# An attention kernel's last addition of an image ahead of the next image's sums, with its tiles moved by 32 bytes

## The chip, the cores and the metric

The kernel runs on one core of a Trainium2 chip. The metric is the device time of one execution in microseconds. A core has a matrix engine (TensorE, PE in the profile; its weight loads are listed as PEld), a vector engine (VectorE, DVE), a scalar engine (ScalarE, ACT), GpSimd (POOL) and SyncE (SP). Each engine works through its own list of instructions, and they wait for each other through semaphores. SBUF is the working memory, of 128 partitions; PSUM holds TensorE's results.

## The reference

Four images `x` of 64 × 64 positions and 256 channels go through one self-attention layer, in float32:

```python
q = einsum('bwhc,cd->bwhd', x, Wq) + bq        # 256 -> 128
k = einsum('bwhc,cd->bwhd', x, Wk) + bk        # 256 -> 128
v = einsum('bwhc,cd->bwhd', x, Wv) + bv        # 256 -> 256
pq, pk, pv = (t.reshape(B, -1, N) for t in (q, k, v))    # N = 4096
energy = einsum('bcn,bcm->bnm', pq, pk)
out = einsum('bcm,bnm->bcn', pv, softmax(energy, axis=-1))
return gamma * out.reshape(B, W, H, C) + x
```

The output has the shape of `x`, (4, 64, 64, 256).

## The kernel before

Matrix products of the attention run in `float32r`, TensorE's one-pass float32 format, with each operand split into parts so that the sum of three products keeps the precision. The projections and the transposes run in plain float32. For one image the kernel projects 16 tiles of `x` to `q`, `k` and `v`, then takes 128 steps `u`: 16 groups `g` of 256 columns, with 8 steps `t` in a group. In a step TensorE multiplies the energies of a step ahead (12 matmuls) and attends (24 matmuls into the banks `a0`, `a1` and `bb`).

When a group ends, its result must be finished: the two accumulators are copied out on ACT (L385), the sums of the softmax are turned into factors, `bb` is added (L400), the sum is scaled (L403), transposed by TensorE (L411), added to `x` and stored. This is a generator, so that its parts fall between the instructions of the steps that follow. A call of `proceed` lets every open generator do one part, up to its next `yield`.

```python
def attend(b, u):
    ...                                     # 24 matmuls into acc[0], acc[1], bb
    if t == NU - 1 and (b, g) != (B - 1, NG - 1):
        o = now["o"] = work.tile([P, NJ, C + 2], F32, tag="o", ...)
        for j in range(NJ):                 # L385, ACT
            nc.scalar.activation(o[:, j, :], acc[j], AF.Identity, scale=1.0 + E)

def finish(b, g, o, bb, xr):
    yield
    yield
    nc.vector.tensor_copy(zall[:, b * NG + g, :], o[:, :, C])                 # L398, DVE
    r, _ = factors(b, g, gam1)                                                # L390, L391, DVE
    nc.vector.tensor_tensor(o[:, :, :C], o[:, :, :C], bb, ALU.add)            # L400, DVE
    yield
    for j in range(NJ):                                                       # L403, ACT
        nc.scalar.activation(o[:, j, :C], o[:, j, :C], AF.Identity, scale=r[:, j : j + 1])
    yield
    yield
    tp = ps_t.tile([P, 2, NB], F32, tag="t", ...)
    ...                                     # L411: 4 transposes on TensorE
    yield
    nc.vector.tensor_tensor(xr, xr, tp, ALU.add)                              # L415, DVE
    nc.gpsimd.dma_start(ov[b, g], xr)
```

The projection of an image: `transposed` turns a tile of `x` (L124, TensorE) and copies it to `xts` (L130, ACT); `project_qk` multiplies (L137, TensorE), adds the biases (`qks`, L146, DVE), and makes three parts `f` of `k` (L263 on ACT, L265 twice on DVE). The loop over the images, with the passage from one to the next:

```python
for b in range(B):
    pr = images[b]
    if b == 0:
        ...                                 # the first image's first tiles
    for i in range(1, NI):
        if i == 3:
            now["banks"] = outputs
        if i + 1 < NI:
            pr.transposed(i + 1)
        while i == 1 and active:            # the rest of the last group's finish
            proceed()
        begin(b, i)
        project_qk(b, i)
        ...
        project_v(b, i - 1)
        proceed()
    project_v(b, NI - 1)
    for u in range(STEPS):
        ...                                 # a step; images[b + 1].transposed(0) in its last but one
        attend(b, u)
        if ...:
            ...
        elif t == NU - 1:
            start(finish(b, g, now["o"], now["bb"], loads.pop((b, "x", g))))
        proceed()
    if b + 1 < B:
        images[b + 1].transposed(1)
        project_qk(b + 1, 0)
```

Tiles get their SBUF addresses in the order in which the pools are opened. Small pools named `pad` hold nothing and move what comes after them:

```python
xpool, xtpool, qkv = pool("xpool", 3), pool("xtpool", 3), pool("qkv", 1)

pool("pad", 1).tile([P, 16], F32, name="pad")
ppool = pool("ppool", 2)                    # probabilities: x, y, h, l, d
pool("pad2", 1).tile([P, 112], F32, name="pad2")
work = pool("work", 2)                      # qks, v4, qr, q, o, r
pool("pad3", 1).tile([P, 48], F32, name="pad3")
kpool = pool("kpool", 3)                    # f, k
```

The constants (`ident`, the weights and biases, `zall`) lie in front of `xpool`.

Of the kernel before, what the change touches and what calls it, by code (L numbers as in the profile page):

```python
# [9 lines left out]
F32 = mybir.dt.float32  # L10
# [10 lines left out]
def kernel(  # L21
# [38 lines left out]
    P = 128  # L60
# [19 lines left out]
    def load_x(pool, b, g):  # L80
        t = pool.tile([P, 2, XB], F32, tag="x", name=f"x_{b}_{g}")
        nc.sync.dma_start(t, xv[b, g])
        return t
# [117 lines left out]
    with ExitStack() as fast:  # L201
        fast.enter_context(tc.manual_schedule())
        pool = lambda name, bufs, **kw: fast.enter_context(
            tc.tile_pool(name=name, bufs=bufs, **kw)
        )
        xpool, xtpool, qkv = pool("xpool", 3), pool("xtpool", 3), pool("qkv", 1)

        pool("pad", 1).tile([P, 16], F32, name="pad")
        ppool = pool("ppool", 2)
        pool("pad2", 1).tile([P, 112], F32, name="pad2")  # L210
# [25 lines left out]
        def proceed():  # L236
            for pieces in list(active):
                if next(pieces, StopIteration) is StopIteration:
                    active.remove(pieces)

        def image(b):
            def xt_out(i):
                return xtpool.tile([P, KC, 2, P], F32, tag="xt", name=f"xts_{b}_{i}")

            def qk_out(i):
                now["qk"] = work.tile([P, 2, 2 * C2], F32, tag="qk", name=f"qks_{b}_{i}")
                return ((now["qk"], 0),)

            def v_out(i):
                now["v4"] = work.tile([P, KC, C], F32, tag="v4", name=f"v4_{b}_{i}")  # L250
                return now["v4"], bv4_sb, 1.0 / E

            images.append(Projection(b, xpool, lambda: next(now["banks"]), xt_out, qk_out, v_out))

            for g in range(NG):
                qd[b, g] = dram.tile([P, NJ, P], F32, tag=f"qd{g}", name=f"qd_{b}_{g}")
            for t in range(NU):
                kf[b, t] = dram.tile([P, 2, 2, 3 * P], F32R, tag=f"kf{t}", name=f"kf_{b}_{t}")

        def halved(f, x):  # L260

            h = f[:, :, 0, :]
            nc.scalar.activation(h, x, AF.Identity, scale=UPPER / 64)  # L263
            for j, s, op in ((1, -64.0, ALU.add), (2, 64.0 * (1.0 + E), ALU.subtract)):
                nc.vector.scalar_tensor_tensor(  # L265
                    f[:, :, j, :], h.bitcast(F32), s, x, ALU.mult, op
                )

        def project_qk(b, i):
            images[b].qk(i)  # L270
            x = now["qk"]
            for s in range(2):
                nc.gpsimd.dma_start(qd[b, i // 2 + NG // 2 * s][:, i % 2, :], x[:, s, :C2])  # L273
            f = kpool.tile([P, 2, 3, P], F32R, tag="f", name=f"f_{b}_{i}", bufs=2)
            halved(f, x[:, :, C2:])
            nc.gpsimd.dma_start(kf[b, i // 2][:, i % 2], f.rearrange("p s j d -> p s (j d)"))

        def project_v(b, i):
            images[b].v(i)
            units[b, "v4", i] = now["v4"]  # L280
            if i < NI - 2:
                halve_v(b, i)
# [12 lines left out]
        def load_q(b, g):  # L295
            t = work.tile([P, NJ, P], F32, tag="qr", name=f"qr_{b}_{g}", bufs=1)
            nc.sync.dma_start(t, qd[b, g])
            loads[b, "qr", g] = t
# [12 lines left out]
        def energy(b, u, k):  # L311

            g, t = divmod(u, NU)
            if k == 0:
                x = ppool.tile([P, 4, NB], F32, tag="x", name=f"x_{b}_{u}", bufs=3)
                y = ppool.tile([P, 4, NB], F32, tag="y", name=f"y_{b}_{u}")
                units[b, u] = x, y
            x, y = units[b, u]
            q, kt = loads[b, "q", g], loads[b, "k", u]
            sa = ps_s.tile([P, 2, NJ, P], F32, tag="a", name=f"sa_{b}_{u}_{k}")  # L320
            sb = ps_s.tile([P, 2, NJ, P], F32, tag="b", name=f"sb_{b}_{u}_{k}")
            for i in range(2):
                for to, f, first, last in ((sa, 0, True, False), (sa, 1, False, True), (sb, 2, True, True)):
                    nc.tensor.matmul(  # L324
                        to[:, i], kt[:, 2 * k + i, f, :], q[:, f], start=first, stop=last
                    )
            for to, sp, scale in ((x, sa, (1.0 + E) / E), (y, sb, -1.0 / E)):
                nc.scalar.activation(  # L328
                    to[:, 2 * k : 2 * k + 2, :],
                    sp.rearrange("p i j d -> p i (j d)"),  # L330
                    AF.Exp,
                    scale=scale,
                )
# [12 lines left out]
        def halves(b, u):  # L346
            x, h = units[b, u]
            l = ppool.tile([P, 4, NB], F32R, tag="l", name=f"l_{b}_{u}")
            nc.vector.tensor_tensor(l, x, h.bitcast(F32), ALU.subtract)  # L349

            d = ppool.tile([P, 4, NB], F32R, tag="d", name=f"d_{b}_{u}")
            nc.vector.scalar_tensor_tensor(  # L352
                d, h.bitcast(F32), 1.0 + E, x, ALU.mult, ALU.subtract
            )
            units[b, u] = h, l, d
# [106 lines left out]
        def begin(b, i):  # L462

            if i == 5:
                load_q(b, 0)
            if i == 9:
                halve_q(b, 0)
            if i in (4, 6, 8):
                load_k(b, i // 2 - 2)
            if i >= 10:  # L470
                energy(b, (i - 10) // 2, i % 2)
            if i in (12, 14):
                join(b, i // 2 - 6)
            if i in (13, 15):
                upper(b, i // 2 - 6)
                load_k(b, i // 2 - 3)

        image(0)
# [3 lines that stand above are left out]
                now["banks"] = energies  # L482
                pr.transposed(0)
                pr.transposed(1)
                project_qk(b, 0)
# [5 lines that stand above are left out]
                while i == 1 and active:  # L491
# [3 lines that stand above are left out]
                if i == NI - 1:  # L495
                    halves(b, 0)
# [4 lines that stand above are left out]
                g, t = divmod(u, NU)  # L501
                ahead = u + LOOK
                if ahead // NU + 1 < NG and ahead % NU == 3:
                    load_q(b, ahead // NU + 1)
                if u == STEPS - NU and b + 1 < B:
                    image(b + 1)
                if u >= STEPS - 3 and b + 1 < B:
                    now["banks"] = energies
                    if u == STEPS - 3:
                        images[b + 1].load(0)  # L510
                    elif u == STEPS - 2:
                        images[b + 1].transposed(0)
                if t == NU - 3:
                    loads[b, "x", g] = load_x(xpool, b, g)
                for k in range(2):
                    if ahead < STEPS:
                        energy(b, ahead, k)
                    if k == 0 and u + 2 < STEPS:
                        join(b, u + 2)
                        upper(b, u + 2)  # L520
                load_k(b, ahead + 2)
                proceed()
                if u + 1 < STEPS:
                    halves(b, u + 1)
                if ahead // NU + 1 < NG and ahead % NU == 5:
                    halve_q(b, ahead // NU + 1)

                if u in (1, 3):
                    halve_v(b, NI - 2 + u // 2)
                attend(b, u)  # L530
                if (b, u) == (B - 1, STEPS - 1):
                    finish_last(b, g, loads.pop((b, "x", g)))
                elif t == NU - 1:
                    start(finish(b, g, now["o"], now["bb"], loads.pop((b, "x", g))))
                proceed()
            if b + 1 < B:
                images[b + 1].transposed(1)
                project_qk(b + 1, 0)

    NB = 512  # L540
    NG = N // NB
# [3 lines left out]
    with tc.If(nc.values_load(again[0:1, 0:1]) > 0), ExitStack() as general:  # L545
        pool = lambda name, bufs, **kw: general.enter_context(
            tc.tile_pool(name=name, bufs=bufs, **kw)
        )
# [125 lines left out]
```

## Time and profile before

| | |
|---|---|
| time, median of 3 | 2474.3 us (2473.92 to 2475.12) |
| span of the profiled execution | 2471.3 us |
| attention matmuls: energies (L324) and attend (L374), float32r | 6,144 and 12,288 |
| mean duration of one attend matmul, `a` from `vh`; `bb` | 283 ns; 279 ns |
| projection matmul records (L137, L158), float32 | 512 and 512 |
| HBM read, written | 445.25 MB, 50.33 MB |
| mean busy share of the DMA engines over the slices | 0.6 to 0.7 in most |

Matmuls are pipelined, so the duration of one (279 ns) is not what it adds to the time: the distance from one start to the next is about 113 to 125 ns. A float32 projection matmul has two records. The three passages between images lie at about 616, 1229 and 1846 us of the span.

### The profile page before, as it was taken

To read this page: it belongs to the slowest core of one execution; us is meant where nothing else is said; L and a number is where in the kernel's file an instruction comes from. 1 tells how busy PE (TensorE), PEld (TensorE's weight loads), DVE (VectorE), ACT (ScalarE), POOL (GpSimd) and SP (SyncE) were. 2 spreads that over 40 slices of the span, in tenths; PEclk is the share of its full clock that TensorE was granted. 3 is DMA by queue.
4 is the path that set the end of the run, shared out by engine and by line. 5 is a ranking of instruction groups with operands and counts; after the bars stand their busy time and mean duration, and the time that the engine had idled before them with its cause. 6 is when DMAs were issued, how large, how long until landed. Compare 5 with 4: busy or idle time off the path is not lost.

```text
span 2471.3 us, 50024 instructions
## 1 busy us (share of the span) xinstructions
PE 2447.6 (99%) x19982; PEld 2412.5 (98%) x19982; DVE 2095.9 (85%) x2314; ACT 1805.7 (73%) x3201; POOL 425.7 (17%) x781
## 2 busy tenths in 40 slices
PE   9999999999999999999999999999999999999998
PEld 8999999999899999999989999999998999999998
DVE  5888888888698888888769888888876988888887
ACT  5777777776677777777657777777766777777775
POOL 4211111111411111111131111111114111111110
PEclk9999999999999999999999999999999999999999
DMA  7666666664766666666477666666647766666663
GB/s 234 220 204 204 208 206 205 198 211 144 237 215 198 206 210 204 207 202 207 142 226 216 204 201 209 204 211 201 207 141 224 224 205 198 208 206 205 209 201 111
DMA packets 137408, 498.92 MB, mean 202 GB/s; under 512 B 15536, under 2 KB 57264, under 8 KB 137168
## 3 DMA queue, kind: packets, MB, share of 16 engines
q0 software_dynamic: 92320, 453.17, 58.8%
q1 hardware_dynamic: 44304, 42.22, 5.6%
q8 instruction: 160, 2.62, 0.4%
q14 instruction: 80, 0.66, 0.1%
q10 hardware_dynamic: 544, 0.26, 0.0%
HBM read 445.25 MB, written 50.33 MB: 201 GB/s over the span
## 4 chain that ended last, share of the span: by engine, by line


## 5 line engine op out<-in xcount | busy, mean ns | idle before, releaser
L328 ACT ACTIVATE x<-sa 128x512 f32<-128x512 f32 x1024 | 612.9, 599 | 494.9 <-PE sa L324 491.7
L338 DVE TENSOR_TENSOR x<-x,y 128x1024 f32<-128x1024 f32 x512 | 626.4, 1223 | 188.0 <-ACT y L328 188.0
L324 PE MATMUL sa<-q,k 128*128 128x256 f32 x4096 | 736.6, 279 | 1.1 <-ACT x L328 1.1
L352 DVE SCALAR_TENSOR_TENSOR d<-h,x 128x1024 fp32r<-128x1024 f32 x512 | 624.4, 1219 | 0.0
L349 DVE TENSOR_TENSOR l<-x,h 128x1024 fp32r<-128x1024 f32 x512 | 624.3, 1219 | 0.0
L324 PEld LDWEIGHTS sa<-q,k 128*128 128x128 f32 x4096 | 619.5, 188 | 2.4 <-ACT x L328 1.9
L328 ACT ACTIVATE y<-sb 128x512 f32<-128x512 f32 x1024 | 614.6, 600 | 0.0
L374 PE MATMUL a<-vh,h 128*128 128x258 f32 x4096 | 574.4, 283 | 0.0
L374 PE MATMUL a<-vl,l 128*128 128x258 f32 x4096 | 572.8, 282 | 0.0
L324 PE MATMUL sb<-q,k 128*128 128x256 f32 x2048 | 567.6, 277 | 0.0
L343 ACT ACTIVATE h<-x 128x1024 fp32r<-128x1024 f32 x512 | 544.6, 1064 | 23.1 <-DVE x L338 19.2
L374 PE MATMUL bb<-vd,d 128*128 128x256 f32 x4096 | 558.6, 279 | 0.0
L308 POOL DMA_DIRECT2D k<-kf x512 | 280.0, 547 | 1575.4 <-PE sb L324 1550.4
L374 PEld LDWEIGHTS a<-vl,l 128*128 128x128 f32 x4096 | 525.3, 189 | 0.0
L374 PEld LDWEIGHTS a<-vh,h 128*128 128x128 f32 x4096 | 522.9, 189 | 0.0
L374 PEld LDWEIGHTS bb<-vd,d 128*128 128x128 f32 x4096 | 515.1, 188 | 0.0
L324 PEld LDWEIGHTS sb<-q,k 128*128 128x128 f32 x2048 | 384.5, 188 | 0.9 <-ACT y L328 0.8
L137 PE MATMUL qk<-wqk_sb,xts 128*128 128x256 f32 x512 | 124.4, 387 | 0.0
L158 PE MATMUL v<-xts,wv_sb 128*128 128x256 f32 x512 | 121.2, 381 | 0.0
L158 PEld LDWEIGHTS v<-xts,wv_sb 128*128 128x128 f32 x512 | 98.2, 192 | 13.7
L137 PEld LDWEIGHTS qk<-wqk_sb,xts 128*128 128x128 f32 x512 | 94.5, 194 | 10.7
L273 POOL DMA_DIRECT2D qd<-qks x128 | 69.1, 544 | 187.3 <-DVE qks L146 178.1
(56 smaller groups left out, 869.7 us busy)
## 6 DMA issues: line engine op xcount, KB each, us to landing
k<-kf POOLq DMA_DIRECT2D x512, 768.0 KB, 4.7
x<-in_x_dram SPq DMA_DIRECT2D x128, 256.0 KB, 3.4
kf<-f POOLq DMA_DIRECT2D x64, 384.0 KB, 3.7
out_dram<-x POOLq DMA_DIRECT2D x63, 256.0 KB, 2.5
qd<-qks POOLq DMA_DIRECT2D x128, 64.0 KB, 2.8
qr<-qd SPq DMA_DIRECT2D x64, 128.0 KB, 2.6
wv_sb<-in_L_conv_Wv_dram POOLq DMA_DIRECT2D x1, 256.0 KB, 5.8
out_dram<-x SPq DMA_DIRECT2D x1, 256.0 KB, 3.7
```

What stands on the lines that cost most here:

```text
L137: nc.tensor.matmul(qk[:, s, :], self.xt[i][:, k, s, :], wqk_sb[:, k, :], start=(k == 0), stop=(k == KC - 1),)
L158: nc.tensor.matmul(vp[:, eh, :], wv_sb[:, k, eh * P : (eh + 1) * P], self.xt[i][:, k].rearrange("p s a -> p (s a)"), start=(k == 0), stop= ...
L273: nc.gpsimd.dma_start(qd[b, i // 2 + NG // 2 * s][:, i % 2, :], x[:, s, :C2])
L308: nc.gpsimd.dma_start(t.rearrange("p (i s) f d -> p i s (f d)", s=2), kf[b, u % NU])
L324: nc.tensor.matmul(to[:, i], kt[:, 2 * k + i, f, :], q[:, f], start=first, stop=last)
L328: nc.scalar.activation(to[:, 2 * k : 2 * k + 2, :], sp.rearrange("p i j d -> p i (j d)"), AF.Exp, scale=scale,)
L338: nc.vector.tensor_tensor(x, x, y, ALU.mult)
L343: nc.scalar.activation(h, units[b, u], AF.Identity, scale=UPPER)
L349: nc.vector.tensor_tensor(l, x, h.bitcast(F32), ALU.subtract)
L352: nc.vector.scalar_tensor_tensor(d, h.bitcast(F32), 1.0 + E, x, ALU.mult, ALU.subtract)
L374: nc.tensor.matmul(out_, left[:, i, j * P : (j + 1) * P], right[:, m, : out_.shape[1]], start=(t == i == 0 and (left is h or left is d and ...
```

## The change

Two calls of `proceed` are added at the passage to the next image: one before the next image's tile 1 is transposed, one after its tile 0 is projected. With the first, the part of `finish` that makes the factors and adds the shared bank `bb` stands ahead of the next image's bias sums in DVE's list. With the second, the scaling stands ahead of the following copy in ACT's list. The purpose is that DVE does this work while it has nothing else to do, so that the last output transposes can run sooner. The `while` loop in the next image then finds two parts fewer to do.

Besides, a pool `pad0` of 8 floats for each partition is opened ahead of `xpool`. It moves every tile from `x` on by 32 bytes, while the constants stay.

```diff
         pool = lambda name, bufs, **kw: fast.enter_context(
             tc.tile_pool(name=name, bufs=bufs, **kw)
         )
+
+
+        pool("pad0", 1).tile([P, 8], F32, name="pad0")
         xpool, xtpool, qkv = pool("xpool", 3), pool("xtpool", 3), pool("qkv", 1)
-
         pool("pad", 1).tile([P, 16], F32, name="pad")
         ppool = pool("ppool", 2)
         pool("pad2", 1).tile([P, 112], F32, name="pad2")
@@ -534,8 +536,10 @@
                     start(finish(b, g, now["o"], now["bb"], loads.pop((b, "x", g))))
                 proceed()
             if b + 1 < B:
+                proceed()
                 images[b + 1].transposed(1)
                 project_qk(b + 1, 0)
+                proceed()
```

## The prediction

> **What bounds the kernel now.** I read the page first, its busy shares and its clock row:
>
> ```profile
> PE 2447.6 (99%) x19982; PEld 2412.5 (98%) x19982; DVE 2095.9 (85%) x2314; ACT 1805.7 (73%) x3201; POOL 425.7 (17%) x781
> ...
> PEclk9999999999999999999999999999999999999999
> ```
>
> TensorE has work for 2447.6 of 2471.3 us, and the other engines have slack. So a gain comes either from the 23.7 us in which TensorE idles or from faster matmuls. The page's chain of waits is empty here, so next I asked for TensorE's own waits. Two of the answer's lines are shown here; the others are a first load, a start, four short waits for ACT and one wait at the very end:
>
> ```profile
> PE ot L411 <- ACT o L403: 10.0, 3, 3.3
> ...
> PE sa L324 <- ACT x L328: 1.1, 4, 0.3
> ```
>
> Three waits of 3.3 us, one at each passage from one image to the next, are the one large idle time that the program order can change. The timeline of the first passage shows what TensorE, DVE and ACT do there (columns: start, duration, engine, line, operation, and in brackets the idle time before it with what ended it):
>
> ```profile
> 616.12 0.60 PE L124 MATMUL xt<-ident,x 128*128 128x128 f32 x4
> 616.55 1.89 PE L137 MATMUL qk<-wqk_sb,xts 128*128 128x256 f32 x8
> 618.28 0.60 PE L124 MATMUL xt<-ident,x 128*128 128x128 f32 x4
> 622.21 0.95 PE L411 MATMUL ot<-ident,o 128*128 128x128 f32 x4 [3.33 <-ACT o L403]
> ```
>
> ```profile
> 618.48 0.69 DVE L146 TENSOR_TENSOR qks<-qk,bqk_sb 128x512 f32<-128x512 f32 x1 [6.00 <-PE qk L137]
> 619.66 0.76 DVE L265 SCALAR_TENSOR_TENSOR f<-f,qks 128x256 fp32r<-128x256 f32 x2 [0.48 <-ACT f L263]
> ...
> 620.88 0.68 DVE L400 TENSOR_TENSOR o<-o,bb 128x512 f32<-128x512 f32 x1
> ```
>
> ```profile
> 614.91 0.87 ACT L385 ACTIVATE o<-a 128x258 f32<-128x258 f32 x2 [3.69 <-PE a L374]
> 616.75 0.59 ACT L130 COPY xts<-xt 128x512 f32<-128x512 f32 x1 [0.98 <-PE xt L124]
> 619.21 0.42 ACT L263 ACTIVATE f<-qks 128x256 fp32r<-128x256 f32 x1 [1.87 <-DVE qks L146]
> 619.53 0.57 ACT L130 COPY xts<-xt 128x512 f32<-128x512 f32 x1
> 621.65 0.91 ACT L403 ACTIVATE o<-o,r 128x256 f32<-128x256 f32 x2 [1.55 <-DVE o L400]
> ```
>
> The old image's `o` is ready at 615.78 (L385) and its `bb` at about 616.3, when the last attend matmuls end. DVE has been idle since 612.5, but its next instruction in order is `qks` of the new image, which waits for TensorE until 618.48. The small operations on `zall` and `r` and the addition `o+bb` (L400) stand behind it and start only at 620.34. L403 scales `o` on ACT after that, and TensorE's output transposes wait for L403.
>
> At the second passage the same gap has a sequel. TensorE's timeline there reads:
>
> ```profile
> 1235.56 1.31 PE L411 MATMUL ot<-ident,o 128*128 128x128 f32 x4 [3.33 <-ACT o L403]
> 1236.65 3.62 PE L137 MATMUL qk<-wqk_sb,xts 128*128 128x256 f32 x8
> 1240.07 2.78 PE L158 MATMUL v<-xts,wv_sb 128*128 128x256 f32 x8
> ```
>
> The eight `qk` records take 3.62 us there against 1.89 at the first passage: the trace's clock record grants half speed for 6.8 us after the second gap, for 3.4 us after the third, and none is lost after the first.
>
> **What the Trainium skill says.** "TensorE: Matmul & The Clock Gate", table at its head: DVE and ACT run a strict first-in-first-out queue. The trace agrees: L398 to L400 had their inputs by about 616.3 and stood 4 us behind `qks`. The same page, "Part 1: The HAM clock gate", has TensorE's clock gate watch windows of 3.4 us and halve the clock after an idle one. The gaps here are 3.33 us, and two of three were followed by half speed in pieces of 3.4 us: the trace agrees in kind. "SBUF — State Buffer", "Operand start alignment", gives only the legality of a start address and says that it timed nothing, so no page tells what 32 bytes are worth for speed.
>
> **The order, worked out.** The compared instruction orders show TensorE's, the DMA queues' and GpSimd's sequences unchanged. At each of three passages the DVE operations L398, L390, L391 and L400 move ahead of `qks` and the two `f`, and on ACT the two L403 move ahead of the copy of `xts` that starts at 619.53. Nothing is added or removed.
>
> - DVE: the `zall` copy starts at about 615.8, when L385 ends. Copy, reciprocal and product took 0.54 us (620.34 to 620.88), so L400 starts when both these and `bb` are done, about 616.4, and ends about 617.1. `qks` still starts at 618.48: no collision.
> - ACT: L403 now stands behind `f` (L263) and ahead of the `xts` copy. It still comes after `f`, which comes after `qks`: so it doesn't start at 617.3 but takes the place of the copy, 619.53. It started at 621.65, so it is 2.12 us earlier.
> - TensorE: the output transposes follow L403's start by 0.56 us (622.21 − 621.65), so they start at 620.09. The transposes before them end at 618.88 (622.21 − 3.33), so a gap of 1.21 us remains out of 3.33.
> - The moved `xts` copy runs from 620.44 to 621.0. The next `qk` doesn't use it (it uses the tile copied at 616.75), and the one that does comes some 4 us later. Its banks are free. So TensorE keeps the 2.12 us.
>
> Three passages by 2.12 give 6.4 us. The clock: at the second passage the output transposes cost 1.31 − 0.95 = 0.36, `qk` 3.62 − 1.89 = 1.73 and `v` 2.78 − 1.89 = 0.89, together 2.98 us. At the third the timeline has 1.07 and 3.50 for the first two, 0.12 + 1.61 = 1.73. A gap of 1.2 us is barely a third of such a window, so I expect no half clock: 4.7 us more. Together 11.1 us, and 2474.3 − 11.1 = 2463.2.
>
> **The 32 bytes, worked out as far as they go.** From the programs' addresses: `x` of the image, `xts`, `vh`, `vl`, `vd`, `q` start at 32 modulo 64 and move to 0 modulo 64 (one of the two buffers of `o` goes the other way); the probabilities' tiles and `k` go from 96 to 128 modulo 256. Constants (`wqk_sb`, `wv_sb`, `ident`) stay. Start to start, the 18,432 fp32r matmuls take 117.0 ns on average by the trace, with a floor of 113: an excess of 4 ns, or 74 us in all. That excess is not noise. At one place of the eight-step cycle the same matmul repeats within 1 or 2 ns in nearly all of its 64 occurrences, while neighbouring places lie anywhere from 113 to 125. So something fixed, such as addresses, sets it, and a shift could redraw it.
>
> What speaks for little effect: the relations among all moved tiles are kept. Rows of `vh` are 1040 bytes apart, so as moving operands they already start at 0, 16, 32 and 48 modulo 64, and their means are 120.0, 119.4, 120.4 and 119.8 ns: alignment modulo 64 buys nothing there. For fp32, `v` has weights at 0 modulo 64 and `qk` at 32, and both take 216 ns. Not covered is an fp32r weight load, which before the change always starts at 32 modulo 64. I put the shift at −2 us, with about ±8 (a tenth of the excess either way): a guess with its size from the trace. The prediction is 2461 us.
>
> **Rivals.**
> - The shift decides. If aligned weights brought all fp32r matmuls near the floor, up to 74 us would go and the time be near 2400. For it: the fixed pattern of 113 to 125 ns. Against it: the two comparisons above. An unlucky redraw by +1 ns per matmul costs 18 us, which makes 2481.
> - The wait only changes its name. L403 waits for `f`, hence for `qks`, hence for `qk`: that is why I don't take the whole 3.33 us. If the moved copy held up `qk` after all, TensorE would wait 0.2 us at each passage, and 2462 results.
> - The gap is closed wholly: 3 × 1.21 = 3.6 us more, 2457. ACT's order speaks against it.
> - The half clock stays after a short gap, or falls elsewhere: up to 4.7 us back, 2466.
>
> **Range and chances.** The order's part lies between 6 and 12 us, the shift's mostly between −10 and +6. Together 2449 to 2469 should hold the time 8 times in 10. 2% is 49 us: faster by that needs nearly the whole matmul excess to go (0.03), slower needs almost 3 ns more on every matmul (0.01).
>
> **What would show it right or wrong.** In the changed kernel TensorE's waits for L403 should total about 3.6 us in three, with L400 starting about 0.6 us after L385's end and L403 right behind `f`. The clock row should show no half speed between images. The means of the large matmul groups and their start-to-start times should stay within 0.5 ns: a step of the mean pitch by 1 ns is 18 us and would make the shift the main cause. A new wait at `qk` or at the later `xts` would show the order's part wrong.

## The result and the profile after

The changed kernel takes 2464.24 us (median of 4 runs, 2463.92 to 2465.16), the kernel before 2474.11 us (4 runs): a ratio of 0.9961 with a 95% interval of 0.9943 to 0.9978. That is 9.9 us less, where about 13 were predicted: 11.1 for the order and 2 for the shift. It lies inside the predicted range of 2449 to 2469.

Line numbers of the passages are two higher in the changed kernel (L403 is now L405, and so on). TensorE's waits by the changed kernel's profile (us in total, times, longest):

```profile
PE ot L413 <- ACT o L405: 3.6, 3, 1.2
```

Before it stood at 10.0 us. The first passage in the changed kernel's timeline, TensorE's, DVE's and ACT's:

```profile
619.00 1.89 PE L137 MATMUL qk<-wqk_sb,xts 128*128 128x256 f32 x8
620.73 0.60 PE L124 MATMUL xt<-ident,x 128*128 128x128 f32 x4
622.52 0.95 PE L413 MATMUL ot<-ident,o 128*128 128x128 f32 x4 [1.20 <-ACT o L405]
623.30 1.89 PE L137 MATMUL qk<-wqk_sb,xts 128*128 128x256 f32 x8
```

```profile
618.24 0.17 DVE L400 COPY zall<-o 128x2 f32<-128x2 f32 x1 [3.36 <-ACT o L387]
...
618.76 0.69 DVE L402 TENSOR_TENSOR o<-o,bb 128x512 f32<-128x512 f32 x1
620.93 0.69 DVE L146 TENSOR_TENSOR qks<-qk,bqk_sb 128x512 f32<-128x512 f32 x1 [1.48 <-PE qk L137]
```

```profile
617.33 0.88 ACT L387 ACTIVATE o<-a 128x258 f32<-128x258 f32 x2 [3.73 <-PE a L376]
619.20 0.59 ACT L130 COPY xts<-xt 128x512 f32<-128x512 f32 x1 [0.99 <-PE xt L124]
621.65 0.42 ACT L265 ACTIVATE f<-qks 128x256 fp32r<-128x256 f32 x1 [1.87 <-DVE qks L146]
621.98 0.89 ACT L405 ACTIVATE o<-o,r 128x256 f32<-128x256 f32 x2
622.77 0.56 ACT L130 COPY xts<-xt 128x512 f32<-128x512 f32 x1
```

DVE adds `bb` at 618.76, some 2 us ahead of the new sums. The sum is ready at 619.45, but ACT takes it up only at 621.98: ahead of the scaling in ACT's list stands `f`, for which ACT waits 1.87 us, until the new sums are there. So 1.2 us of the wait stay. The second passage, where the kernel before ran at half speed:

```profile
1233.82 0.95 PE L413 MATMUL ot<-ident,o 128*128 128x128 f32 x4 [1.19 <-ACT o L405]
1234.61 1.89 PE L137 MATMUL qk<-wqk_sb,xts 128*128 128x256 f32 x8
```

The eight `qk` records take 1.89 us here, full speed; they took 3.62 before. In the changed kernel's profile no passage is followed by half speed.

The two profiled spans differ by less than the timed runs: 2471.3 and 2463.2, 8.1 us. Matched matmul by matmul, the changed kernel's execution loses 2.3 us in its first 11.5 us, where its projection records start 0.43 us apart instead of 0.21 (the clock at the start of the program). It then gains 6.4 us at the passages (three times 2.13) and 4.6 us by the half speed that is gone; 0.7 us is lost in small steps elsewhere. A start of that kind came and went from profile to profile.

### The profile page after: what moved, and what is told of

Its sections match the earlier page's. It is cut to its first block, busy times and chain, and to the rows that moved or that the text cites. A ratio compares the mean times of both kernels' runs of the same rounds, so it can differ in the third digit from the quotient of the medians.

```text
span 2463.2 us, 50024 instructions
## 1 busy us (share of the span) xinstructions
PE 2445.7 (99%) x19982; PEld 2411.2 (98%) x19982; DVE 2096.1 (85%) x2314; ACT 1804.0 (73%) x3201; POOL 425.7 (17%) x781
## 4 chain that ended last, share of the span: by engine, by line
## 5 line engine op out<-in xcount | busy, mean ns | idle before, releaser
L158 PE MATMUL v<-xts,wv_sb 128*128 128x256 f32 x512 | 120.3, 379 | 0.0
```

The costliest lines, as they stand in the source:

```text
L158: nc.tensor.matmul(vp[:, eh, :], wv_sb[:, k, eh * P : (eh + 1) * P], self.xt[i][:, k].rearrange("p s a -> p (s a)"), start=(k == 0), stop= ...
```

## Experiments

Theory A: the order does it all, the shift nothing. Theory B: the shift has a share of its own, through the addresses of TensorE's operands. Times are compared with runs of the kernel before in the same batch. Those had a median of 2475.3 us in the batch of the first four experiments, 2474.9 in that of the next four, and 2474.6 in the last.

### Each part alone

The order without the shift, and then the shift without the order, both as edits of the changed kernel:

```diff
-        pool("pad0", 1).tile([P, 8], F32, name="pad0")
```

> The two added calls without the 32 bytes: all tiles lie where they lay before. Theory A (the order does it all: a wait of 3.33 us falls to 1.2 us at each of three passages, and the half clock after them goes): 2464.2 us, within 1 us of the changed kernel, with three waits of the output transposes for ACT of 1.2 us each. Theory B (the shift has a share): it differs from 2464.2 by what the shift is worth, over 2 us.

Measured: 2464.19 us, ratio 0.9955 (0.9941 to 0.9968), and three waits of 1.2 us. Theory A's number.

```diff
             if b + 1 < B:
-                proceed()
                 images[b + 1].transposed(1)
                 project_qk(b + 1, 0)
-                proceed()
```

> The 32 bytes without the two calls. Theory A: as the kernel before, 2474.1 us within 1 us, three waits of 3.3 us, and every group of attention matmuls at the same mean distance from start to start as before (117.0 ns where none waits). Theory B: it differs by over 2 us, and the distances with it.

Measured: 2476.68 us, ratio 1.0007 (0.9999 to 1.0015). Its waits are those of the kernel before:

```profile
PE ot L413 <- ACT o L405: 10.0, 3, 3.3
```

The median is 1.4 us above the kernel before, where less than 1 was expected; the interval of the ratio includes 1. Its profile has half speed for 3.4 us after all three gaps. Start to start, the attention matmuls that don't wait (under 140 ns) take 117.05 ns on average, against 117.03 before. To see whether a cost of 1.4 us is real, the changed kernel and its twin without the shift were run side by side once more:

> The changed kernel once more, on the same chip as its twin without the 32 bytes in the next run. Both theories of the order: about 2464.2 us. If the shift is worth nothing, the two lie within 1 us of each other; the first comparison of the shift alone gave +1.4 us with an interval that holds zero, and a true cost of that size would show again here.

> The two calls without the 32 bytes, beside the changed kernel. No effect of the shift: the same within 1 us. A cost of the shift of about 1.4 us: this one faster by that.

Measured: 2464.67 us (ratio 0.9958, 0.9945 to 0.9972) with the shift and 2464.03 us (0.9956, 0.9942 to 0.9969) without. The 1.4 us don't come back; what is left, 0.6 us, is less than the spread of either (1.6 and 2.6 us). The traces show below where such a cost arises.

### What remains of the wait

The second added call taken away again:

```diff
                 project_qk(b + 1, 0)
-                proceed()
```

> The changed kernel without its second added call: DVE's addition is early, but ACT's scaling stands behind the copy of the transposed tile (0.57 us) again. Theory A (the rest of the wait is ACT's order): the three waits grow from 1.2 to about 1.77 us, the time by 1.7 us to 2465.9. Rival (DVE's early addition alone is enough, ACT's place is of no account): as the changed kernel, 2464.2.

Measured: 2468.01 us, ratio 0.9972 (0.9962 to 0.9982). At the first passage, TensorE and ACT:

```profile
621.74 0.94 PE L413 MATMUL ot<-ident,o 128*128 128x128 f32 x4 [1.68 <-ACT o L405]
```

```profile
620.39 0.42 ACT L265 ACTIVATE f<-qks 128x256 fp32r<-128x256 f32 x1 [1.87 <-DVE qks L146]
620.72 0.57 ACT L130 COPY xts<-xt 128x512 f32<-128x512 f32 x1
621.18 0.91 ACT L405 ACTIVATE o<-o,r 128x256 f32<-128x256 f32 x2
```

The wait is 1.68 us, near the 1.77 expected, since the copy stands ahead of the scaling again. So the second call is worth 0.5 us of wait at each passage, 1.4 us in all. The time, though, is 3.8 us above the order alone in the same batch, where 1.7 was expected. At the second passage this profile shows half speed again (3.17 us for eight `qk`):

```profile
1233.66 0.94 PE L413 MATMUL ot<-ident,o 128*128 128x128 f32 x4 [1.68 <-ACT o L405]
1234.44 3.17 PE L137 MATMUL qk<-wqk_sb,xts 128*128 128x256 f32 x8
```

That costs 1.28 us on these `qk` and 0.45 us on the `v` that follow, 1.7 us together. It happened at one of three passages in the profiled execution. The other runs fit: all nine have a mean granted clock (the share of full speed that TensorE was granted over the span) of 0.997 or 0.998, and all five of the order alone have 0.999. A thousandth of the span is 2.5 us, so half speed can make up the rest of the difference; the record doesn't say at which passages it fell in each run.

The other way round, the second call is put ahead of the projection, so that ACT scales before it makes `f`:

```diff
                 images[b + 1].transposed(1)
-                project_qk(b + 1, 0)
                 proceed()
+                project_qk(b + 1, 0)
```

> The second added call moved ahead of the projection of the next image's tile 0: ACT scales before it makes f, which waits for the new projection's sums. Theory A: the scaling starts at 0.1 us after the addition or the copy of the transposed tile and is done before TensorE has finished the following transposes; the three waits of 1.2 us go wholly, 3.6 us less than the changed kernel, 2460.6. Rival (another wait takes its place, at the projection that follows or at the bank of the transposes): TensorE's waits at the passages stay above 0.3 us each and the gain is under 2.5 us.

Measured: 2460.23 us (2457.64 to 2461.07), ratio 0.9939 (0.9926 to 0.9953), 4.0 us under the order alone in the same batch. TensorE's list of waits has no entry for the output transposes at the passages any more. The first passage, TensorE and ACT:

```profile
618.63 0.60 PE L124 MATMUL xt<-ident,x 128*128 128x128 f32 x4
619.07 0.60 PE L413 MATMUL ot<-ident,o 128*128 128x128 f32 x4
619.50 1.89 PE L137 MATMUL qk<-wqk_sb,xts 128*128 128x256 f32 x8
```

```profile
617.10 0.58 ACT L130 COPY xts<-xt 128x512 f32<-128x512 f32 x1 [1.00 <-PE xt L124]
617.59 0.91 ACT L405 ACTIVATE o<-o,r 128x256 f32<-128x256 f32 x2
619.56 0.42 ACT L265 ACTIVATE f<-qks 128x256 fp32r<-128x256 f32 x1 [1.07 <-DVE qks L146]
```

The scaling fills time in which ACT waited, and the transposes follow without a gap. They also take 0.43 us from start to the next `qk` instead of 0.79: the second of the four transposes starts 0.11 us after the first, against 0.41 before, so it seems to wait no longer for the second scaling. The same order without the 32 bytes:

> The best order found, the second added call ahead of the projection, without the 32 bytes. If the shift is worth nothing: 2460 us as with it, within 1.5 us, and no wait of the output transposes at the three passages.

Measured: 2459.12 us (2457.55 to 2459.45), ratio 0.9937 (0.9920 to 0.9953). With the shift it was 2460.23 us in another batch; the two ratios, 0.9937 and 0.9939, can't be told apart.

### Why the shift does next to nothing

For each of the three attend groups (`vh`, `vl`, `vd`), each step of the cycle of eight and the first seven of its eight matmuls, I took the median distance to the next start over its 64 occurrences: 168 places, with the kernel before as the standard. In the changed kernel all 168 agree within 1 ns. The question is then whether addresses matter at all. Further edits of the changed kernel, one for each run:

```diff
-        pool("pad0", 1).tile([P, 8], F32, name="pad0")
+        pool("pad0", 1).tile([P, 40], F32, name="pad0")     # shift_160: all by 160 bytes
-        pool("pad", 1).tile([P, 16], F32, name="pad")
+        pool("pad", 1).tile([P, 24], F32, name="pad")       # pad_24; pad_8 has 8 instead
-    VC = C + 4
+    VC = C + 2                                              # vc_258
```

> The changed kernel with all tiles from x on moved by 160 bytes instead of 32: every relation among the moved tiles is kept, every absolute address is another. If only the relations count, all 168 compared places of the attend matmuls keep their medians within 1 ns and the time is 2464 to 2466 us. If the change's 32 bytes were harmless by luck, places move and the time goes up by over 3 us.

> The changed kernel with the empty pool between the v tiles and the probabilities enlarged from 64 to 96 bytes: now the weights of the attend matmuls move by 32 bytes against their moving operand, which the change itself never does. If the fixed pattern of 113 to 125 ns from start to start comes from where the two operands lie against each other, the medians of many of its 192 places move by over 2 ns; if it comes from something else (the order of the instructions), they stay, and the time is 2464 to 2466 us.

> The changed kernel with the empty pool between the v tiles and the probabilities cut from 64 to 32 bytes, the opposite of the run with 96. If the relation of the two operands counts: under half of the 168 places stay within 1 ns, and the time leaves 2464 us by over 3 us, more probably upward, since the pools had been chosen by their times. If 96 bytes were bad for another reason (an end of memory, one tile's place): 2464 to 2466 us and the places stay.

> The changed kernel with rows of vh and vl of 258 instead of 260 elements, 1032 bytes apart instead of 1040: [...]everything after it moves up. If addresses set the pattern, the places of vh and vl get other medians while those of vd keep theirs; if the 258 columns themselves cost the 120 ns against 113 to 116 for 256, the mean of vh and vl stays at 119.5 to 120.

| kernel (one run each, the first: median of 4) | us | places within 1 ns of before | over 2 ns off | mean distance, not waiting |
|---|---|---|---|---|
| changed kernel | 2464.2 | 168 | 0 | 117.06 ns |
| all by 160 bytes | 2464.8 | 168 | 0 | 117.05 ns |
| 96 bytes between `vd` and the probabilities | 2487.0 | 44 | 99 | 118.25 ns |
| 32 bytes between them | 2491.0 | 41 | 95 | 118.59 ns |
| rows of `vh`, `vl` of 258 | 2473.0 | 45 | 96 | 117.47 ns |

The four single runs have a mean granted clock of 0.999, and the widest set of runs of one kernel, 21 of the kernel before, spans 5.1 us.

Moving everything by the same amount leaves every place as it was. Resizing `pad` moves the weights (`h`, `l`, `d`), and all else behind it, `q` and `k` too, by 32 bytes against `x`, `xts` and the moving operands (`vh`, `vl`, `vd`) ahead of it; that costs 23 to 27 us. With 32 bytes between, the tiles behind `pad` lie exactly where they lay in the kernel before, and the tiles ahead of it where they lie in the changed kernel, so neither place is bad by itself. The fixed pattern does come from addresses, from where things lie against each other, and the change keeps those relations. That the two which count are weights and moving operand is the nearest reading; other pairs across `pad` were not tested apart.

How directly this holds can be seen in single rows. One step further, `vh` and `vl` are read 2 × 1040 = 2080 bytes on, which is 2048 + 32. With 96 bytes between, the weights lie 32 bytes further on, so step `t` stands as step `t − 1` did, but for 2048 bytes. The medians for `vh` (ns, first seven matmuls):

```
changed kernel, t = 0:   114 119 123 120 117 122 121
96 bytes,       t = 1:   114 119 123 120 118 122 121
changed kernel, t = 2:   120 122 113 119 122 120 125
96 bytes,       t = 3:   120 122 113 119 122 120 125
```

The same fits for `vl`. With 96 bytes, four of the seven steps that have a predecessor fit so (`t` = 1, 3, 4 and 5, at least six of seven places within 1 ns), and `t` = 2, 6 and 7 don't. With 32 bytes `t = 0` takes the changed kernel's `t = 1` in all seven places of `vh` and of `vl`, but no other step fits in both. Two steps taken at random agree in about two of seven places. So a relation modulo 2048 seems to be a part of the rule, and it isn't the whole. What happens in the memory was not found out.

One part surprised. The energies' operands `q` and `k` move together in all these runs, yet they slow down as well. A step and the energies after it in the changed kernel, then the same with 32 bytes between (columns as above; the distance between starts is what counts):

```profile
327.06 1.08 PE L376 MATMUL bb<-vd,d 128*128 128x256 f32 x8
327.98 0.39 PE L326 MATMUL sa<-q,k 128*128 128x256 f32 x2
...
329.34 1.11 PE L376 MATMUL a<-vh,h 128*128 128x258 f32 x8
```

```profile
328.53 1.11 PE L376 MATMUL bb<-vd,d 128*128 128x256 f32 x8
329.48 0.41 PE L326 MATMUL sa<-q,k 128*128 128x256 f32 x2
...
330.90 1.13 PE L376 MATMUL a<-vh,h 128*128 128x258 f32 x8
```

The eight `bb` take 0.92 us in the first and 0.95 in the second, the twelve energies 1.36 us (113 ns each) and 1.42 us (118 ns each). In the run with 32 bytes `q` and `k` lie at the very addresses of the kernel before, so their own place is not the reason. The changed kernel's trace has both paces too; its next step:

```profile
331.25 1.11 PE L376 MATMUL bb<-vd,d 128*128 128x256 f32 x8
332.20 0.40 PE L326 MATMUL sa<-q,k 128*128 128x256 f32 x2
...
333.61 1.12 PE L376 MATMUL a<-vh,h 128*128 128x258 f32 x8
```

Here the twelve take 1.41 us. They do so after step `t = 3` in all 64 cases, whichever buffers of `q` and `k` they read, and the last `bb` of that step run at 118 ns as well. After other steps with nothing in between, the last `bb` and the energies run at 113 in nearly all cases (after `t = 1` at 118). So the pace of the matmuls ahead carries on into the energies. Transposes in between break it: in the kernel before, the energies behind `t = 1` take 113 ns in all 60 cases in which output transposes stand in between, and 118 in three of the four without.

So the cost of moving tiles against each other doesn't stay where the relation changed. By the mean distances, of about 22 us with 96 bytes the `bb` matmuls bear 11, the energies 10 and `vl` 1; of about 28 us with 32 bytes the energies bear 17, `bb` 9 and `vl` 2. `vh` bears none: its places change, and their mean stays at 119.8 ns. The carried pace would also tell why `vd`'s places moved in the run with rows of 258 (33 of 56 by over 2 ns) though `vd` and `d` moved by the same 512 bytes there: my expectation that they keep theirs was wrong.

It is also where the shift does cost something. The output transposes read `ident`, which the shift doesn't move. The 60 groups of energies behind them take 75.0 us together in each of the four profiles without the shift, and 75.7 in each of the five with 32 bytes: 28 of the 60 groups are slower. That is about 0.65 us, near the 0.6 that the runs side by side left. That `ident`'s relation is the reason is inferred.

## Why the prediction was right, and where not

**The bound and the wait.** Right. TensorE's three waits fell from 3.33 to 1.20 us each, where 1.21 was worked out. DVE's addition starts 0.55 us after the accumulators are copied out, where 0.6 was expected, and the scaling follows `f` without idle time. From the second transposes of `xt` to the next `qk`, the first passage took 4.72 us before (618.28 to 623.00) and takes 2.57, so TensorE keeps the gap's 2.13 us; no wait at `qk` or at the later `xts` took its place. The kernel before had there:

```profile
623.00 1.89 PE L137 MATMUL qk<-wqk_sb,xts 128*128 128x256 f32 x8
```

The step that saw ACT's order as the new limit is what the two moved calls show: 1.68 us of wait with the copy ahead of the scaling, none with the scaling ahead of `f`.

**The clock.** Right in kind. Eight profiles with gaps of 1.2 us have no half speed after any of 24 gaps; the kernel before has it after two of three gaps of 3.3 us and the shift alone after three of three; gaps of 1.7 us have it after one of three. "TensorE: Matmul & The Clock Gate", "Part 1: The HAM clock gate", in the Trainium skill gives a window of 3.4 us and an idle one as the cause. The window agrees: inside every trace the clock record changes at steps of 3.41 us. But no gap here is as long as a window, so a window idle in part was enough. Laid over these steps, half speed began behind all five windows in which a gap took 1.97 to 2.86 us, behind one of the three in which it took 1.67 to 1.75 us, and behind none in which it took less. Once it stayed for a second window, which isn't explained. So the length alone doesn't decide: the first gap of the kernel before fell on a boundary, 1.75 us on one side and 1.58 on the other, and escaped by its place.

The 4.7 us were read from one execution, but the timed runs fit them. The mean granted clock of a run is 0.996 or 0.997 in 36 of 37 runs of the kernel before beside the experiments, and 0.998 or 0.999 in all 19 of the changed kernel and of the order alone. The means, 0.9963 and 0.9986, differ by some 5 to 6 us of the span (an estimate from rounded figures).

**The order's sum.** 11.1 us predicted. The order alone measured 11.1 us in the batch of the first four experiments (2475.29 − 2464.19) and 10.8 in the second (2474.86 − 2464.03); the changed kernel had 9.9 and 10.2. That the first agrees to a tenth is partly luck, since the batches differ by more and the clock's part came from one execution.

**The shift.** The term of the sum that was mis-sized: −2 us, with −10 to +6 in the range, was put down, and it is about +0.65 us by the traces, and 0.6 by the medians of the runs side by side, which is within their spread. The prediction had the argument that decides it, "the relations among all moved tiles are kept", and set a guess beside it all the same, because the excess of 74 us over the floor could be redrawn. It can, by 23 to 27 us with 32 bytes, but in these runs only where tiles moved against each other. The comparison of alignments, too, was thinner than it looked: it used `vh` alone, and `vl`, with the same four starts modulo 64, has 119.9, 119.9, 117.9 and 120.3 ns. The mean distance moved by 0.03 ns where a limit of 0.5 had been set.

**The rivals.** None came: the shift didn't decide, no new wait arose, and in the profiles of the changed kernel the half clock didn't stay. "The gap is closed wholly" was rejected for ACT's order, and changing that order closes it.

## What to carry to other kernels

When one engine is busy 99% of the span, look at its few waits one by one and at the in-order neighbours of the instruction it waits for: here an addition and a scaling stood behind work for the next stage that had to wait itself, and adding two calls gave 10 us, another place for the second of them 4 more. Removing a gap on TensorE can be worth more than its length, because the slow clock behind it can go too: here 4.7 us beside 6.4. A pad that moves everything together is no experiment on addresses; if layout is to be tuned, move a matmul's weights against its moving operand, expect losses as well, and compare the whole step, since the pace carries on into matmuls that were not touched.

## What was not expected

- Moving the tiles behind `pad`, the attend matmuls' weights among them, by 32 bytes against the moving operands cost 23 us (96 bytes between instead of 64) and 27 us (32 bytes), about 1% of the time, with the same instructions in the same order.
- Matmuls whose own operands kept their relation slowed down with them: the energies of a step from 113 to 118 ns each.
- Half speed followed one of three gaps of only 1.7 us, and failed to follow one of 3.3 us that fell across two windows of the clock.
